# Layers 1 to 3 of a graph network: the adjacency's transpose by block loads and VectorE, the mask and the scaling placed elsewhere in the round

## The chip, the cores and the metric

The kernel runs on one core of a Trainium2 chip. A core has five engines with a queue of instructions each: TensorE (PE, with PEld for its weight loads), VectorE (DVE), ScalarE (ACT), GpSimd (POOL) and SyncE (SP, which here issues nearly all DMAs). They work side by side and wait for each other through semaphores. The metric is the time of one execution on the device in microseconds (us). The kernel before took 3421.11 us, the median of 3 runs (3419.83 to 3423.85).

## The reference

There are 64 graphs of 256 nodes with 256 features in f32, and one adjacency matrix `adj` per graph (256x256, most entries zero, the diagonal kept). Four layers follow each other, and each ends in a residual addition and a layer norm:

```python
# layer 0: a scan over the 256 nodes, a gated recurrence
x = _layernorm(x + _L0_gnn_ref(x, adj, ...), axis=-1)
# layer 1: relu(D^-1/2 adj D^-1/2 (x W^T + b))
degree = jnp.sum(adj_matrix, axis=-1)
norm_adj = adj_matrix * d_inv_sqrt[:, :, None] * d_inv_sqrt[:, None, :]
output = jax.nn.relu(jnp.einsum('bnm,bmo->bno', norm_adj, transformed))
# layer 2: one attention head
att = jax.nn.softmax(scores * mask - NEG * (1.0 - mask), axis=2)
out = jax.nn.relu(jnp.einsum('bnh,ho->bno', jnp.einsum('bnm,bmh->bnh', att, v), Wo) + bo)
# layer 3: eight heads of 32 features, masked where adj is not above 0
scores = jnp.where(adj[:, None, :, :] > 0, scores, jnp.float32(NEG))
attn = jax.nn.softmax(scores, axis=-1)
```

Layer 1's product contracts over the columns of `adj`, and layer 3's scores are kept with keys on the partitions. Both therefore use the transpose of `adj`: layer 1 scaled by `d_inv_sqrt`, layer 3 as a mask.

## The kernel before

Layer 0 is a recurrence over all 64 graphs at once (`_recurrence`). It leaves its states in DRAM as `Hd`, and takes the first 1508 us of the profiled execution. The function `_layers` then does layers 1 to 3 graph by graph. A tile of a graph is 128 partitions by 2 by 256: rows c*128 to c*128+127 are chunk c.

The work is a software pipeline over graphs, written out by hand. A list `ROUND` names steps as `who.step.argument`, and every instruction is issued in that order on its engine; no scheduler changes it (`manual_schedule`). In round `t` the letter tells the graph: L is graph t+1 (degrees, first norm, transpose of `adj`), A is graph t (layer 1), B is t-1 (layer 2), C is t-2 (layer 3 up to the exponentials), E is t-3 (layer 3's output, last norm, store). At the head of round `t` the loads of graph t+2 are issued from SP: `xin` (x), `ad` (adj), `y` (Hd). An engine works through its own queue in order, so an instruction that waits holds all behind it.

Steps that matter here, with lines:

- `residual_0` (L1040): POOL adds `xin` to `y`. `norm_a` (L948 to L952): VectorE's statistics and POOL's power; `norm_b` (L958, L960): VectorE's `shift`, ScalarE's scaling of `y`.
- `degrees_a`, `degrees_b` (L1052 to L1062): row sums of `ad` to the power -1/2, `dis`.
- `adT` (L1064 to L1073), the last but one step of a round: four PE transposes of `ad` into a PSUM bank (`flipped`, L986), two ScalarE activations that scale them into `adT`, and VectorE's mask `neg3`, which reads the same bank.
- `xT` (L1076): PE transposes of `y` and ScalarE's copy. The steps `A.xT.1` and `B.xT.2` open a round and `C.xT.3` stands in its middle.
- `g` (L1085): PE's product with `adT`, ScalarE's relu with `dis`, POOL's addition to `y` (L1092).
- `s2` and `exp2` (L1120, L1130): layer 2's scores, VectorE's `sm` (L1124) and row maximum (L1010), ScalarE's exponentials (L1017).
- `f2` (L1140): a PE product, two VectorE operations from its PSUM bank into the SBUF tile `f` (L1144), a third from `f` and `y` into `y` (L1148).
- `s3` (L1170): for four heads at a time PE's scores, VectorE's addition of the mask (`p`, L1189), ScalarE's exponentials (L1190), and POOL's sum of the two chunks (`p3s`, L1192).
- `o3` (L1196): PE's sums over the keys (L1206, reading `p3s`) and its products with v (L1215), in the order sums of the first four heads, products, sums of the last four. `d3` divides (L1229 to L1231).
- `f3` (L1236): a PE product and VectorE's addition to `y` (L1238). `bias_3` (L1160): SP writes `y` to `Yd`, then POOL adds a bias to `y` (L1162). `store` (L1240) writes the output.

The PSUM banks of `flipped` and `product` are one ring of four (`bank`, L965): a taker waits until the one four before it has been read.

Of the kernel before, what the change touches and what calls it, by code (L numbers as in the profile page):

```python
# [9 lines left out]
F32 = mybir.dt.float32  # L10
BF16 = mybir.dt.bfloat16
AF = mybir.ActivationFunctionType
ALU = mybir.AluOpType
AX = mybir.AxisListType

NEG = 9000000000000000.0
# [3 lines left out]
P = 128  # L20
# [890 lines left out]
def _layers(tc, ident, Hd, Yd, x, adj, weights, out):  # L911
# [8 lines left out]
    nc = tc.nc  # L920
    nat, W2, W3, b1_r, b2_r, b3_r, cols = weights
    B, N, D = x.shape
# [5 lines left out]
    with ExitStack() as ctx:  # L928
# [9 lines left out]
        io = ctx.enter_context(tc.tile_pool(name="l_io", bufs=3))  # L938
# [26 lines left out]
        def bank(name, shape=(P, 2, D)):  # L965
            return ps.tile(list(shape), F32, tag="mm", name=name, bufs=4)

        for c in range(2):
            pt = bank(f"w1_{c}", (P, 2, P))
# [11 lines left out]
        def flipped(src, t):  # L981

            pt = bank(f"tr_{t}")
            for a in range(2):
                for c in range(2):
                    nc.tensor.transpose(  # L986
                        pt[:, a, c * P:(c + 1) * P], src[:, c, a * P:(a + 1) * P], ident
                    )
            return pt

        def product(lhsT, rhs, t):

            pm = bank(f"mm_{t}")
            for c in range(2):
                for k in range(2):
                    nc.tensor.matmul(  # L996
                        pm[:, c, :], lhsT[:, k, c * P:(c + 1) * P], rhs[:, k, :],
                        start=(k == 0), stop=(k == 1),
                    )
            return pm  # L1000

        def new(tag, t, bufs=2, shape=(P, 2, D)):
            return work.tile(list(shape), F32, tag=tag, name=f"{tag}_{t}", bufs=bufs)
# [17 lines left out]
        class Graph:  # L1021
# [7 lines left out]
            def load(self):  # L1029
                b = self.b  # L1030
                self.xin = io.tile([P, 2, D], F32, tag="xin", name=f"xin_{b}")
                nc.sync.dma_start(self.xin, x[b].rearrange("(c p) d -> p c d", p=P))
                self.ad = io.tile([P, 2, N], F32, tag="ad", name=f"ad_{b}", bufs=4)
                nc.sync.dma_start(self.ad, adj[b].rearrange("(c p) m -> p c m", p=P))
                self.y = io.tile([P, 2, D], F32, tag="y", name=f"y_{b}", bufs=7)
                nc.sync.dma_start(self.y, Hd[:, b, :].rearrange("(c p) d -> p c d", p=P))

# [23 lines left out]

                nc.vector.tensor_mul(self.dis, self.dis, self.some)  # L1062

            def adT(self):  # L1064
                pt = flipped(self.ad, f"ad_{self.b}")
                self.adT_sb = new("adT", self.b)
                for c in range(2):
                    nc.scalar.activation(
                        self.adT_sb[:, c, :], pt[:, c, :], AF.Copy, scale=self.dis[:, c:c + 1]
                    )  # L1070

                self.neg3 = new("neg3", self.b, 4)
                nc.vector.tensor_scalar(self.neg3, pt, 0.0, -NEG, ALU.is_le, ALU.mult)  # L1073

            def xT(self, l):
                pt = flipped(self.y, f"x{l}_{self.b}")  # L1076
# [62 lines left out]

            def f2(self):  # L1140
                pm = product(self.pT2_sb, self.w2_sb, f"2f_{self.b}")
                f = new("f2", self.b)
                for c in range(2):
                    nc.vector.scalar_tensor_tensor(  # L1144
                        f[:, c, :], pm[:, c, :], self.sums2[:, c:c + 1], b2_r,
                        ALU.mult, ALU.add,
                    )
                nc.vector.scalar_tensor_tensor(self.y, f, 0.0, self.y, ALU.max, ALU.add)  # L1148


            def qk3(self, s):
# [93 lines left out]
        ROUND = """  # L1245
            A.xT.1 B.xT.2 E.o3 E.d3.0 B.qk2.0 C.norm_b.2 E.d3.1
            A.t B.qk2.1 B.v2 L.residual_0 B.masks L.degrees_a
            E.f3 L.degrees_b C.xT.3 A.g C.bias_3 L.norm_a.0
            C.qk3.0 C.qk3.1 E.norm_a.3 A.norm_a.1 L.norm_b.0 B.s2 B.exp2
            C.s3.0 C.v3 B.w2  # L1250
            B.pT2 E.norm_b.3 E.store A.norm_b.1 C.s3.1 B.f2
            L.adT B.norm_a.2
        """.split()
        graphs = [Graph(b) for b in range(B)]
        graphs[0].load()
        for t in range(-1, B + 3):
            if 0 <= t + 2 < B:
                graphs[t + 2].load()
            for step in ROUND:
                who, name, *args = step.split(".")  # L1260
                b = t - "LABCE".index(who) + 1
# [146 lines left out]
def kernel(ctx: ExitStack, tc: tile.TileContext, ins, out):  # L1408
# [25 lines left out]
    )  # L1434
    Yd = dram.tile([B, P, 2, D], F32, name="Yd")
    found = _layers(tc, ident, Hd, Yd, x, adj, weights, out)
    with tc.If(found > 0):
        _layer_3(tc, ident, Yd, adj, l3, out)
# [36 lines left out]
```

## Time and profile before

| | |
|---|---|
| median of 3 runs | 3421.11 us |
| the profiled execution | 3418.97 us, its span 3417.3 us |
| granted TensorE clock, mean | 0.984 |
| PE busy | 3201.3 us (94%) |
| VectorE busy | 2545.1 us (74%) |
| POOL busy | 1874.6 us (55%) |
| ScalarE busy | 1844.0 us (54%) |
| HBM read, written | 224.01 MB, 99.61 MB |

The profile is of one execution. Its page gives each engine's busy time, the span in 40 equal slices with a digit for the busy tenths, the DMA queues, the chain of work that ended last, and the costliest groups of instructions. The trace behind it can be asked for windows of time, for the chain, and for a timeline, which has a row per run of equal instructions: start in us, length in us, engine, line, operation, output tile, input tiles, shapes and count. A bracket at the end tells how long the engine was idle before and what released it. Consecutive instructions of an engine may overlap by a few hundredths, so a row's length is not exactly the distance to the next one. SPq is SyncE's queue; its rows are the issuing of a DMA, not the transfer.

### The profile page before, as it was taken

The numbers are of one execution on the slowest core, as the hardware profiler recorded it, in microseconds if no ns is written. First come the engines' busy times: TensorE is split into PE (matmuls) and PEld (weight loads), VectorE is DVE, ScalarE is ACT, GpSimd is POOL, SyncE is SP. The second block draws the span as 40 slices with busy tenths as digits, with TensorE's granted clock in tenths as the row PEclk, the third lists the DMA queues.
The fourth block names the chain that finished last, engine by engine and source line by source line (L and its number), as shares of the span: only waits on it lengthen the run. The fifth ranks groups of instructions, "written<-read, shape, count | busy, mean of one in ns | idle before, by whom it ended". The sixth has DMA issues, their size and how long they took to land.

```text
span 3417.3 us, 78895 instructions
## 1 busy us (share of the span) xinstructions
PE 3201.3 (94%) x28840; PEld 2340.6 (68%) x28840; DVE 2545.1 (74%) x7317; ACT 1844.0 (54%) x4754; POOL 1874.6 (55%) x2165
## 2 busy tenths in 40 slices
PE   5799999999889998969999999999999999999997
PEld 4555555555555555547888888888888888888885
DVE  3477777777667777755887888887888878888875
ACT  0255555454444444435666666666666666666664
POOL 2376777776667777743444444444444444444443
PEclk8999999999999999989999999999999999999999
DMA  9756675788876575231111111111111111111100
GB/s 301 228 158 146 162 191 153 171 196 211 205 185 168 152 175 145 57 97 35 46 47 42 44 45 47 47 47 47 47 47 47 47 47 47 47 47 47 47 29 20
DMA packets 389343, 347.82 MB, mean 102 GB/s; under 512 B 107357, under 2 KB 355305, under 8 KB 383721
## 3 DMA queue, kind: packets, MB, share of 16 engines
q1 hardware_dynamic: 371256, 325.82, 35.6%
q10 hardware_dynamic: 17696, 16.91, 1.5%
q8 instruction: 232, 3.80, 0.5%
q14 instruction: 159, 1.29, 0.1%
HBM read 224.01 MB, written 99.61 MB: 95 GB/s over the span
## 4 chain that ended last, share of the span: by engine, by line
PE 75%; DVE 8%; DMA 7%; ACT 3%; SPq 3%; issue 2%; POOL 1%; DVEq 0%; POOLq 0%; ACTq 0%
PE mm L996 13%; PE rc L605 6%; PE rc L597 4%; PE s L1180 4%; PE mm_2f L996 3%; PE mm_t L996 3%; PE mm_3v L996 3%; PE mm_3f L996 3%; PE mm_2v L996 3%; PE mm_g L996 3%; PE mm_2s L996 3%; PE o L1215 3%; DVE ACC L630 3%; PE mm_2w L996 3%; PE late L521 3%; PE o L1206 3%
## 5 line engine op out<-in xcount | busy, mean ns | idle before, releaser
L1192 POOL TENSOR_TENSOR p3s<-p 128x256 f32<-128x256 f32 x512 | 387.4, 788 | 366.6 <-ACT p L1190 366.4
L630 DVE SCALAR_TENSOR_TENSOR ACC<-keep,S,ACC 128x128 f32<-128x128 f32 x1712 | 479.3, 343 | 36.7 <-POOL ACC L875 30.9
L996 PE MATMUL mm<-xT,weights 128*128 128x256 f32 x2048 | 481.8, 383 | 2.9 <-ACT xT L1078 2.9
L996 PEld LDWEIGHTS mm<-xT,weights 128*128 128x128 f32 x2048 | 384.7, 190 | 79.4 <-issue 25.5
L1189 DVE TENSOR_TENSOR p<-s,neg 128x512 f32<-128x512 f32 x512 | 317.7, 683 | 115.3 <-PE s L1180 115.3
L667 POOL TENSOR_TENSOR ACC<-ACC,far 128x384 f32<-128x384 f32 (+1 forms) x313 | 372.3, 1189 | 24.5
L663 POOL TENSOR_TENSOR far<-hs,S 128x384 f32<-128x384 f32 (+1 forms) x313 | 304.9, 974 | 4.7
L960 ACT ACTIVATE y<-y,shift,rstd 128x256 f32<-128x256 f32 x512 | 273.4, 599 | 48.5 <-DVE shift L958 30.7
L1190 ACT ACTIVATE p<-p 128x512 f32<-128x512 f32 x512 | 295.4, 628 | 2.1 <-DVE p L1189 1.6
L805 POOL TENSOR_TENSOR ready<-ACC,dinv 128x128 f32<-128x128 f32 x255 | 102.3, 401 | 310.7 <-DVE ACC L630 310.4
L597 PE MATMUL rc<-WxT,xqT 128*64 128x256 f32 x2048 | 269.3, 384 | 0.0
L1103 ACT ACTIVATE qk<-mm,weights 128x256 f32<-128x256 f32 x256 | 107.5, 471 | 269.1 <-PE mm L996 269.1
L521 PE MATMUL late<-Hw,An 64*32 64x256 f32 x3840 | 215.7, 388 | 30.2 <-ACT lb L256 26.7
L1092 POOL TENSOR_TENSOR y<-y,g 128x512 f32<-128x512 f32 x64 | 81.1, 1267 | 267.6 <-issue 267.6
L1229 DVE RECIPROCAL rT<-o 128x256 f32<-128x256 f32 x128 | 223.8, 1748 | 0.3 <-PE o L1206 0.2
L952 POOL TENSOR_TENSOR rstd<-rstd,mhalf 128x2 f32<-128x2 f32 x256 | 173.8, 697 | 82.3 <-DVE rstd L951 80.6
L948 DVE BATCH_NORM_STATS2 st<-y 128x6 f32<-128x256 f32 x512 | 209.0, 408 | 13.3 <-POOL y L1092 12.5
L605 PE MATMUL rc<-WhT,rT 128*64 128x128 f32 x2048 | 168.9, 286 | 47.9 <-DVE rT L828 47.2
L824 ACT ACTIVATE rs<-rc 128x128 f32<-128x128 f32 x256 | 71.1, 278 | 256.8 <-PE rc L605 256.8
L828 DVE TENSOR_TENSOR rT<-rT_ps,xpT 128x128 f32<-128x128 f32 x256 | 74.3, 290 | 178.8 <-PE rT_ps L826 177.1
L605 PEld LDWEIGHTS rc<-WhT,rT 128*64 128x64 f32 x2048 | 106.8, 136 | 142.3 <-DVE rT L828 126.5
L614 ACT COPY xpT<-xpT_ps 128x128 f32<-128x128 f32 x256 | 68.2, 266 | 245.8 <-PE xpT_ps L612 245.8
(163 smaller groups left out, 7404.8 us busy)
## 6 DMA issues: line engine op xcount, KB each, us to landing
xX<-in_x_dram ACTq DMA_DIRECT2D x16, 1024.0 KB
Us<-xu SPq DMA_DIRECT2D x64, 256.0 KB
xq<-in_x_dram SPq DMA_DIRECT2D x64, 256.0 KB
ACC<-Us SPq DMA_DIRECT2D x32, 512.0 KB
Es<-eu SPq DMA_DIRECT2D x64, 256.0 KB
early_sb<-Es SPq DMA_DIRECT2D x32, 512.0 KB
xin<-in_x_dram SPq DMA_DIRECT2D x64, 256.0 KB
ad<-in_adj_dram SPq DMA_DIRECT2D x64, 256.0 KB
```

What stands on the lines that cost most here:

```text
L521: nc.tensor.matmul(pb[g][q * T:(q + 1) * T, e, :], An[rows, b].rearrange("p u s -> p (u s)"), Hw[rows, b, :], start=True, stop=True,)
L597: nc.tensor.matmul(G[o * B:(o + 1) * B], xqT[a, i // 2][:, i % 2, kc, h * B:(h + 1) * B], WxT[:, kc, o, gates], start=False, stop=False, s ...
L605: nc.tensor.matmul(G[o * B:(o + 1) * B], hT[:, kc * B:(kc + 1) * B], WhT[:, kc, o, g], start=False, stop=(kc == 1), skip_group_check=True,)
L630: nc.vector.scalar_tensor_tensor(acc[:, 0, :], keep[:, j % 2, :], s, acc[:, 0, :], ALU.mult, ALU.add)
L663: nc.gpsimd.tensor_mul(tmp[:, 0:count, :], hs.unsqueeze(1).to_broadcast(shape), s.unsqueeze(2).to_broadcast(shape),)
L667: nc.gpsimd.tensor_add(acc, acc, tmp[:, 0:count, :])
L960: nc.scalar.activation(y[:, c, :], y[:, c, :], AF.Identity, bias=shift[:, c:c + 1], scale=rstd[:, c:c + 1],)
L996: nc.tensor.matmul(pm[:, c, :], lhsT[:, k, c * P:(c + 1) * P], rhs[:, k, :], start=(k == 0), stop=(k == 1),)
L1189: nc.vector.tensor_add(p, s_ps[i], self.neg3)
L1190: nc.scalar.activation(p, p, AF.Exp, scale=ISQ)
L1192: nc.gpsimd.tensor_add(both, p[:, 0, :], p[:, 1, :])
L1229: nc.vector.reciprocal(rT, o_ps[:, 1, :])
```

## The change

`adj` is loaded a second time, as 32x32 blocks set out so that transposing each block in place gives the whole transpose: eight more DMAs per graph, 32 partitions by 8 runs of 128 bytes each, between `ad` and `y`. VectorE transposes the blocks (`adT_v`) and makes the mask from the result in SBUF, in front of `f3`'s addition. ScalarE scales the result into `adT` (`adT_s`) behind `C.xT.3`'s copy. The four PE transposes and their PSUM bank go. The step `adT` leaves the end of the round. In `f2` the two operations write back to the PSUM bank of the product instead of to an SBUF tile, and the third reads that bank.

```diff
                 nc.sync.dma_start(self.ad, adj[b].rearrange("(c p) m -> p c m", p=P))
+                self.az = io.tile([P, 2, 8, 32], F32, tag="az", name=f"az_{b}", bufs=3)
+                for j in range(4):
+                    for a in range(2):
+                        at = a * P + j * 32
+                        nc.sync.dma_start(
+                            self.az[j * 32:(j + 1) * 32, a],
+                            adj[b, :, at:at + 32].rearrange("(i r) c -> r i c", r=32),
+                        )
                 self.y = io.tile([P, 2, D], F32, tag="y", name=f"y_{b}", bufs=7)
...
-            def adT(self):
-                pt = flipped(self.ad, f"ad_{self.b}")
+            def adT_v(self):
+
+                self.turned = new("adTr", self.b)
+                nc.vector.transpose(
+                    self.turned.rearrange("p a m -> p (a m)"),
+                    self.az.rearrange("p a i c -> p (a i c)"),
+                )
+                self.neg3 = new("neg3", self.b, 4)
+                nc.vector.tensor_scalar(self.neg3, self.turned, 0.0, -NEG, ALU.is_le, ALU.mult)
+
+            def adT_s(self):
                 self.adT_sb = new("adT", self.b)
                 for c in range(2):
                     nc.scalar.activation(
-                        self.adT_sb[:, c, :], pt[:, c, :], AF.Copy, scale=self.dis[:, c:c + 1]
-                    )
-
-                self.neg3 = new("neg3", self.b, 4)
-                nc.vector.tensor_scalar(self.neg3, pt, 0.0, -NEG, ALU.is_le, ALU.mult)
+                        self.adT_sb[:, c, :], self.turned[:, c, :], AF.Copy,
+                        scale=self.dis[:, c:c + 1],
+                    )
...
                 pm = product(self.pT2_sb, self.w2_sb, f"2f_{self.b}")
-                f = new("f2", self.b)
                 for c in range(2):
                     nc.vector.scalar_tensor_tensor(
-                        f[:, c, :], pm[:, c, :], self.sums2[:, c:c + 1], b2_r,
+                        pm[:, c, :], pm[:, c, :], self.sums2[:, c:c + 1], b2_r,
                         ALU.mult, ALU.add,
                     )
-                nc.vector.scalar_tensor_tensor(self.y, f, 0.0, self.y, ALU.max, ALU.add)
+                nc.vector.scalar_tensor_tensor(self.y, pm, 0.0, self.y, ALU.max, ALU.add)
...
             A.xT.1 B.xT.2 E.o3 E.d3.0 B.qk2.0 C.norm_b.2 E.d3.1
             A.t B.qk2.1 B.v2 L.residual_0 B.masks L.degrees_a
-            E.f3 L.degrees_b C.xT.3 A.g C.bias_3 L.norm_a.0
+            L.adT_v E.f3 L.degrees_b C.xT.3 L.adT_s A.g C.bias_3 L.norm_a.0
             C.qk3.0 C.qk3.1 E.norm_a.3 A.norm_a.1 L.norm_b.0 B.s2 B.exp2
             C.s3.0 C.v3 B.w2
             B.pT2 E.norm_b.3 E.store A.norm_b.1 C.s3.1 B.f2
-            L.adT B.norm_a.2
+            B.norm_a.2
```

## The prediction

> **What bounds the kernel now.** I read the page first (busy shares, the slices), then the windows of single rounds, then the chain, then the timeline of one round, engine by engine.
>
> ```profile
> span 3417.3 us, 78895 instructions
> ...
> PE   5799999999889998969999999999999999999997
> ...
> PEclk8999999999999999989999999999999999999999
> ```
>
> The recurrence (layer 0) ends near 1508 us; the rest is layers 1 to 3, where PE is full and the granted clock is 1.0. The diff touches that second part alone. One of its rounds, from the windows (columns: PE, PEld, DVE, ACT, POOL busy, clock, DMA share, GB/s):
>
> ```profile
> 2431.00:2459.86 28.86, 28.86 (x197) 23.30 (x198) 23.28 (x57) 18.42 (x40) 13.77 (x17) 1.00 0.14 47
> ```
>
> The L996 row that opens a round stands at 1593.64 and at 3325.76: 1732.1 us, 60 rounds of 28.87. So a round is what counts. In the chain of waits the adjacency's transposes have this place (start, us, what):
>
> ```profile
> 2453.39 1.92 PE mm_2f L996 x8
> 2455.32 0.44 PE tr_ad L986 x4
> 2455.75 0.87 PE tr_x L986 x8
> 2456.62 0.57 PE o L1206 x8
> ```
>
> But "PE busy 28.86" hides a wait. The timeline of a round's end, all engines:
>
> ```profile
> 2455.12 2.19 ACT L1190 ACTIVATE p<-p 128x512 f32<-128x512 f32 x4
> ...
> 2455.89 3.26 POOL L1192 TENSOR_TENSOR p3s<-p 128x256 f32<-128x256 f32 x4 [2.93 <-ACT p L1190]
> ...
> 2456.71 1.15 DVE L1148 SCALAR_TENSOR_TENSOR y<-f,y 128x512 f32<-128x512 f32 x1
> ...
> 2458.52 0.34 PEld L1206 LDWEIGHTS o<-p3s,ones 128*32 128x32 f32 x6
> ...
> 2459.20 0.14 PEld L1206 LDWEIGHTS o<-p3s,ones 128*32 128x32 f32 x2 [0.34 <-POOL p3s L1192]
> ```
>
> PE reaches the last pair of layer 3's row sums at 2458.86 and stands 0.34 us until POOL's fourth `p3s` ends at 2459.15. A round is therefore a loop: PE from there to the end of `mm_2s` (back to back), VectorE's `sm`, ScalarE without a gap from `exp2` to the four `p`, POOL's four `p3s`, PE again. **A shorter PE alone gains nothing; POOL's end must move too.** Cut finer, the third `p3s`:
>
> ```profile
> 2457.27 1.19 POOL L1192 TENSOR_TENSOR p3s<-p 128x256 f32<-128x256 f32 x1
> ```
>
> 1.19 us against a median of 0.73, while L1148 runs on VectorE. L1148 took 0.69 in the first round (1565.19, POOL idle) and 1.15 here. Both read two SBUF tensors; one holds the other up.
>
> **The change, part by part (per round).**
>
> *PE.* The four transposes go: 0.44 us off the stretch in front of the sums.
>
> *f2 in PSUM.* The third operation reads PSUM and one SBUF tensor. Rows of that form (L1189, 128x512) take 0.62 each, four in 2.48, the second four clear of POOL and the first four partly beside POOL's `p3s`, with no difference. So I take 0.69 (uncontended L1148; L1124, PSUM and SBUF, also 0.69) in place of 1.15, and for POOL four `p3s` at the uncontended 2.79 (the round's other four) in place of 3.26: POOL ends 0.48 earlier, at 2458.67. Bounds: 0 (it still collides) and 0.50. The two operations in front now write PSUM: L853 (PSUM out) 359 ns against L866 348, so 0.03 together on VectorE, hidden.
>
> *The loop.* PE would be ready at 2458.86 - 0.44 = 2458.42, POOL is at 2458.67: PE still waits 0.3, and the round shrinks by POOL's 0.48. If POOL came earlier still, PE's own limit would be 0.44 + 0.34 = 0.78; if nothing but PE counted, 0.44.
>
> *adT_v on VectorE.* It gets a 128x512 transpose, of which the trace has no row. Nearest: one-input 128x512 rows (L1052 0.68, L696 0.69); far above, RECIPROCAL, 1748 ns for 256 columns, so 3.5 us. Below nothing is excluded, since it is an added instruction. I take 0.69, the same shape and type with one input. `neg3` from SBUF: 0.69 at most as now (L1073). Together 1.38. The place:
>
> ```profile
> 2438.12 0.17 DVE L1058 TENSOR_SCALAR some<-some 128x2 f32<-128x2 f32 x1
> 2439.84 0.69 DVE L1238 TENSOR_TENSOR y<-y,mm_3f 128x512 f32<-128x512 f32 x1 [1.55 <-PE mm_3f L996]
> ...
> 2447.19 0.69 DVE L1124 TENSOR_TENSOR sm<-mm_2s,ad 128x512 f32<-128x512 f32 x1 [0.86 <-PE mm_2s L996]
> ```
>
> VectorE idles 1.55 just there, and it arrives earlier: `neg3` leaves the round's end (0.69 and a wait of 0.20) and L1148 loses 0.46, 1.35 in all, of which 0.48 is the shorter round. Cover 1.55 + 0.87 = 2.42 against 1.38: cost nothing. Without cover it would hold E's addition, `dis`, ScalarE's `adT_s`, its `g`, POOL's `y`, and at last the `shift` in front of `sm`.
>
> The Trainium skill ("VectorE: DVE Perf Modes", The three transpose paths) gives 311 ns for 128x128 bf16 in 32x32 blocks; four of that, 1.24 us, is an estimate by that page, and its rules for authors send 128x128 transposes to TensorE. By it adT_v is 1.93, still inside 2.42, so the sum stays and only the margin halves.
>
> *adT_s on ScalarE.* 2 x 0.47 in SBUF instead of PSUM, from the round's end (2457.21) to between xT (ends 2440.87) and `g` (2442.01, 1.14 idle before it). `dis` is there at 2440.60. Cost nothing; cover left 0.3, and behind it 0.86 in front of `sm`. What it leaves gives the xT copies 0.8 more room.
>
> *PSUM banks.* One taker less, 16 a round; f2's bank is freed at about 2457.4, its next user four takes on (`t`) starts near 2461. Nothing.
>
> *SP and DMA.* Eight more issues between `ad` and `y`, 256 runs of 128 B each. L269's loads of such runs (`A`) have a median of 0.42 us, so with the gaps 8 x 0.51 = 4.1 us of SP. In a round SP stands idle from 2456.2 to 2463.9, when `Yd` goes out: hidden; behind `Yd` waits POOL's L1162, at 2444.20, 9 us after `Yd`'s 2435.05. The transfer itself, from a stretch of layer 0 of 2 us with almost nothing else:
>
> ```profile
> DMA packets 2505, 0.38 MB, mean 189 GB/s; under 512 B 2493, under 2 KB 2493, under 8 KB 2504
> ```
>
> 2048 runs are so about 1.7 us of a round's 28, beside a DMA share of 0.14.
>
> *The start is where the issues show*, once:
>
> ```profile
> 1509.89 0.46 SPq L1034 DMA_DIRECT2D ad<-in_adj_dram  x1
> 1510.59 0.37 SPq L1036 DMA_DIRECT2D y<-Hd  x1
> ...
> 1515.32 1.26 POOL L1040 TENSOR_TENSOR y<-y,xin 128x512 f32<-128x512 f32 x1 [8.21 <-DMA y<-Hd]
> ```
>
> Graph 0's `y` is issued at about 1514.5 instead of 1510.59. Its data then has no `ad` in front of it, so I take 3.2 of the 3.9 for the landing (bounds 2.5 and 4.1). Against it: `shift` at 1519.53 took 1.21 beside POOL's next L1040, which now comes later (-1.06); `adT` stood in front of xT on ScalarE at 1538.58 (-0.72); at 1564.24 the transposes and `adT` stood in the chain (-0.94). Net +0.5, from -0.2 to +2.5.
>
> **Sum.** 60 rounds x 0.48 = 28.8; the round before them, where PE doesn't wait for POOL, 0.44; the two after the last `ad`, where L1148 still stands beside `p3s`, 0.9; minus 0.5: 29.6 us. The profiled execution took 3418.97 (span 3417.3 and 1.67 around it), so 3389.4. It lay 2.1 under the median of the runs, 3421.11; from the median 3391.5.
>
> **Rivals.**
> 1. *POOL's end does not move* (f2 still collides, or another VectorE instruction takes L1148's place beside `p3s`). PE then waits 0.78 at the sums and rounds stay 28.87: 3421.1 + 0.5 = 3421.6, no change. For it: VectorE's L951, one input, also stretched to 1.28 beside a POOL addition (2442.99). Against: what now follows f2 beside `p3s` is statistics of one input, which keep 0.42 in every row. Chance 0.06.
> 2. *The transpose costs RECIPROCAL's rate*, 3.5 us. adT_v 4.2 against 2.42 makes E's addition 1.8 late; `adT_s` and `g` absorb 0.6, `sm`'s idle time 0.86: 0.35 a round is lost, 21 us: 3412. Chance 0.05.
> 3. *Slower: SP becomes the bound.* If an `az` issue took what `raw`'s took at 141.37, 2.04 us, SP would be at `Yd` at 2472.1, `Yd` would land (2.8 as `xin` did) near 2475.3, and POOL's L1162, due at 2472.6, would be 2.7 late; 0.86 is spare before `sm`: +1.9 a round, 3500. It decides from about 1.86 us an issue on. Against: `A` 0.42, `S` with 328 KB of such runs 0.63; `raw` was issued into full DMA engines, here their share is 0.14. Chance 0.06. The Trainium skill ("DMA: Bandwidth & Descriptors", Specifications) asks for 512 B and more, below which a write becomes read-modify-write; by it this rival would weigh more. The 2493 small packets in 2 us show no such slowness, so I give it no more weight.
>
> **How the numbers follow.** The forecast has 0.81; its own bounds are rounds of 0.44 to 0.50 and a start of +2.5 to -0.2, so 3389 to 3397 from the median, 3387 to 3399 with the spread of the runs (3419.83 to 3423.85). 0.02 remains for what I don't see, on the slow side with rival 3 in part. A measurement tells about 0.2% (7 us) from no change. Faster 0.87 (forecast, rival 2, remainder), same 0.06 (rival 1), slower 0.07. The range reaches a little towards rival 2: 3385 to 3403.
>
> **What would show it.** Right: `tr_ad` gone; rounds of 28.4; L1162 of the new file (f2's third) near 0.69 and four `p3s` near 2.8; PEld still waiting 0.2 to 0.3 on POOL at L1220; transpose and mask done before `mm_3f` ends; ScalarE idle before `g`; SP issues of about 0.45; the first POOL `y` some 3 us later. Wrong: a wait of 0.8 at the sums (rival 1), E's addition waiting for nothing and `sm` late (2), L1176 waiting for `Yd` (3).

## The result and the profile after

The kernel after takes **3390.91 us** (median of 4 runs, 3389.4 to 3393.05), the kernel before, on the same chip, 3422.48 (median of 4, 3419.83 to 3424.96). The ratio is **0.9903, 95% interval 0.989 to 0.9916**: 1% faster. The forecast was 3391.5 in a range of 3385 to 3403.

The profiled execution took 3390.03 (span 3388.2) against 3418.97 before, 28.9 less. By stages, from the rows that bound them in the two traces (the last `hs` of layer 0, and the L996 rows that open rounds):

| stretch | before, us | after, us | difference | forecast |
|---|---|---|---|---|
| to the end of layer 0 | 1507.80 | 1508.87 | +1.1 | 0 |
| start, to the first full round | 85.84 | 86.29 | +0.4 | +0.1 |
| 60 full rounds | 1732.1 | 1700.9 | -31.2 | -28.8 |
| the last three rounds and the end | 91.5 | 92.2 | +0.7 | -0.9 |

So the gain is in the rounds and nowhere else: 28.35 us each instead of 28.87. One round, from the windows of the kernel after (PE, PEld, DVE, ACT, POOL busy with their counts, clock, DMA share, GB/s):

```profile
2417.32:2445.66 28.34, 28.34 (x193) 22.94 (x193) 23.44 (x59) 18.30 (x40) 13.32 (x18) 1.00 0.22 59
```

The DMA share went from 0.14 to 0.22, which is the eight block loads (it is 0.15 in a round of the kernel below that has `f2` in PSUM without them, and 0.22 in the one that has them alone). The end of the same round in the chain of waits, where `tr_ad` is gone:

```profile
2439.74 1.92 PE mm_2f L996 x8
2441.66 0.87 PE tr_x L986 x8
2442.53 0.57 PE o L1220 x8
2443.10 1.73 PE o L1229 x32
2444.83 0.83 PE o L1220 x8
```

And in the timeline, all engines:

```profile
2442.17 2.82 POOL L1206 TENSOR_TENSOR p3s<-p 128x256 f32<-128x256 f32 x4 [2.90 <-ACT p L1204]
...
2443.20 0.69 DVE L1162 SCALAR_TENSOR_TENSOR y<-mm_2f,y 128x512 f32<-128x512 f32 x1
...
2444.43 0.34 PEld L1220 LDWEIGHTS o<-p3s,ones 128*32 128x32 f32 x6
2445.04 0.14 PEld L1220 LDWEIGHTS o<-p3s,ones 128*32 128x32 f32 x2 [0.27 <-POOL p3s L1206]
```

`f2`'s third operation takes 0.69 instead of 1.15 and the four `p3s` 2.82 instead of 3.26; the longest of the 512 `p3s` is now 0.757. The two operations in front of it, which now write PSUM, take 1.01 instead of 0.86, and nothing waits for that. PE still waits for the fourth `p3s`, 0.27 instead of 0.34. VectorE and ScalarE at the place to which the transpose moved:

```profile
2452.62 0.71 DVE L1075 STREAM_TRANSPOSE adTr<-az 128x512 f32<-128x512 f32 x1 [0.20 <-issue]
2453.36 0.43 DVE L1080 TENSOR_SCALAR neg<-adTr 128x512 f32<-128x512 f32 x1
2454.53 0.69 DVE L1252 TENSOR_TENSOR y<-y,mm_3f 128x512 f32<-128x512 f32 x1 [0.74 <-PE mm_3f L996]
```

```profile
2455.45 0.91 ACT L1085 ACTIVATE adT<-adTr,dis 128x256 f32<-128x256 f32 x2
2456.69 0.84 ACT L1104 ACTIVATE g<-mm_g,dis 128x256 f32<-128x256 f32 x2 [0.34 <-PE mm_g L996]
```

The transpose takes 0.71 and the mask 0.43, and VectorE still stands 0.74 us idle in front of E's addition: the work is covered, as is `adT_s`, behind which ScalarE has 0.34 left.

### The profile page after: what moved, and what is told of

Its sections match the earlier page's. It is cut to its first block, busy times and chain, and to the rows that moved or that the text cites. A ratio compares the mean times of both kernels' runs of the same rounds, so it can differ in the third digit from the quotient of the medians.

```text
span 3388.2 us, 78957 instructions
## 1 busy us (share of the span) xinstructions
PE 3173.6 (94%) x28584; PEld 2322.8 (69%) x28584; DVE 2556.4 (75%) x7381; ACT 1837.2 (54%) x4754; POOL 1844.3 (54%) x2165
## 4 chain that ended last, share of the span: by engine, by line
PE 75%; DMA 7%; DVE 7%; ACT 3%; SPq 3%; issue 2%; POOL 1%; DVEq 0%; POOLq 0%; ACTq 0%
PE mm L996 14%; PE rc L605 6%; PE s L1194 4%; PE rc L597 4%; PE mm_2f L996 3%; PE mm_3v L996 3%; PE mm_t L996 3%; PE mm_3f L996 3%; PE mm_2v L996 3%; PE mm_g L996 3%; PE mm_2s L996 3%; PE mm_2w L996 3%; PE late L521 3%; PE o L1229 3%; DVE ACC L630 3%; PE tr_x L986 2%
## 5 line engine op out<-in xcount | busy, mean ns | idle before, releaser
L1206 POOL TENSOR_TENSOR p3s<-p 128x256 f32<-128x256 f32 x512 | 358.3, 731 | 366.0 <-ACT p L1204 365.9
L996 PE MATMUL mm<-xT,weights 128*128 128x256 f32 x2048 | 484.4, 385 | 2.7 <-ACT xT L1093 2.7
L996 PEld LDWEIGHTS mm<-xT,weights 128*128 128x128 f32 x2048 | 387.4, 192 | 79.4 <-issue 25.5
```

Of the source, the lines that this page charges most:

```text
L996: nc.tensor.matmul(pm[:, c, :], lhsT[:, k, c * P:(c + 1) * P], rhs[:, k, :], start=(k == 0), stop=(k == 1),)
L1206: nc.gpsimd.tensor_add(both, p[:, 0, :], p[:, 1, :])
```

## The experiments

"A round" is the mean of 60 from the trace. Layer 0, which no edit touches, ended anywhere between 1505 and 1519 us in the profiled executions, so the rounds tell small differences better than the totals do. In the headings, "after" and "before" are the two kernels. Each ratio is to runs of before on the same chip.

### Which part brought the gain: f2 in PSUM or the transpose?

After, with `f2`'s SBUF tile put back:

```diff
+                f = new("f2", self.b)
...
-                        pm[:, c, :], pm[:, c, :], self.sums2[:, c:c + 1], b2_r,
+                        f[:, c, :], pm[:, c, :], self.sums2[:, c:c + 1], b2_r,
...
-                nc.vector.scalar_tensor_tensor(self.y, pm, 0.0, self.y, ALU.max, ALU.add)
+                nc.vector.scalar_tensor_tensor(self.y, f, 0.0, self.y, ALU.max, ALU.add)
```

> The changed kernel with f2 as it was (third operation from an SBUF tile f); the transposes stay off PE. Theory A (the round is a loop through POOL's p3s, and f2 in PSUM is what moves its end): VectorE's third f2 operation is back at about 1.15 us, four p3s at 3.26, PE waits about 0.8 us at the last row sums instead of 0.27, rounds 28.8 to 28.9 as before the change, total within 5 us of the kernel before. Theory B (PE's transposes were the path, f2 counts for nothing): rounds 28.43, total some 26 us under the kernel before.

Measured: 3417.94 us, ratio to before 0.9985 (0.9976 to 0.9995), a round 28.80. The transposes are off PE, and next to nothing is gained. Timeline of this kernel, end of a round:

```profile
2455.81 3.25 POOL L1207 TENSOR_TENSOR p3s<-p 128x256 f32<-128x256 f32 x4 [2.90 <-ACT p L1205]
...
2456.69 1.09 DVE L1163 SCALAR_TENSOR_TENSOR y<-f,y 128x512 f32<-128x512 f32 x1
...
2459.12 0.14 PEld L1221 LDWEIGHTS o<-p3s,ones 128*32 128x32 f32 x2 [0.55 <-POOL p3s L1207]
```

PE comes 0.44 earlier and stands longer at the last row sums: the bracket has 0.55 instead of 0.34, and the eight matmuls of that group last 1.46 in the timeline instead of 1.08. Those two rows, of this kernel and of before:

```profile
2458.28 1.46 PE L1221 MATMUL o<-p3s,ones 128*32 128x256 f32 x8
```

```profile
2458.74 1.08 PE L1206 MATMUL o<-p3s,ones 128*32 128x256 f32 x8
```

Those 0.38 and the 0.07 that the round did shrink by make up the 0.44. The other half, before with `f2` alone changed:

```diff
                 pm = product(self.pT2_sb, self.w2_sb, f"2f_{self.b}")
-                f = new("f2", self.b)
...
-                        f[:, c, :], pm[:, c, :], self.sums2[:, c:c + 1], b2_r,
+                        pm[:, c, :], pm[:, c, :], self.sums2[:, c:c + 1], b2_r,
...
-                nc.vector.scalar_tensor_tensor(self.y, f, 0.0, self.y, ALU.max, ALU.add)
+                nc.vector.scalar_tensor_tensor(self.y, pm, 0.0, self.y, ALU.max, ALU.add)
```

> The kernel before with only f2 put back to PSUM; adj is still transposed on PE. Theory A: four p3s take 2.8 us, the wait of 0.34 at the last row sums goes, PE then is the limit, rounds 28.53, total some 20 us under the kernel before. Theory B (only PE's own work counts): no change. Theory C (all of POOL's 0.44 counts by itself): rounds 28.43, 26 us.

Measured: 3397.94 us, ratio 0.9926 (0.9909 to 0.9943), a round 28.41. Of the 0.52 that the whole change brings, 0.46 is here. And PE no longer waits; chain of this kernel, then the last row sums in the chain of before:

```profile
2451.98 0.44 PE tr_ad L986 x4
2452.42 0.87 PE tr_x L986 x8
2453.29 0.57 PE o L1205 x8
2453.86 1.73 PE o L1214 x32
2455.59 0.47 PE o L1205 x8
```

```profile
2458.92 0.90 PE o L1206 x8
```

The last row sums take 0.47 here, 0.83 in after and 0.90 in before. That difference is what a late `p3s` costs PE: 0.36 and 0.43, more than the 0.27 and 0.34 that stand in the brackets. Theory A had counted with the bracket's 0.34 and so missed the round by 0.12; the 28.43 of theory C lies nearer, but by it the gain ends with POOL's 0.44 and no other limit, and PE now waits for no `p3s`. The kernel with `norm_b` moved as well, below, tells the two apart.

### If POOL comes still earlier, what are PE's transposes worth?

After, with layer 3's second half of the normalization and its store behind `C.s3.1`, so that ScalarE has two `y` less in front of the second four `p`:

```diff
-            B.pT2 E.norm_b.3 E.store A.norm_b.1 C.s3.1 B.f2
+            B.pT2 A.norm_b.1 C.s3.1 E.norm_b.3 E.store B.f2
```

> The changed kernel with E.norm_b.3 and E.store behind C.s3.1 instead of in front of A.norm_b.1, so ScalarE starts the second four exponentials about 1.0 us earlier. Theory A (POOL's end still holds PE by 0.27): p3s end about 1 us earlier, the wait goes, PE alone is the limit, rounds 28.08, total about 3375. Theory B (PE is the limit already): rounds 28.35, 3391.

Measured: 3368.43 us, ratio to before 0.9846 (0.9829 to 0.9862), a round 27.94. It beats the changed kernel by 0.41 a round, where 0.27 was expected. Timeline and chain of this kernel (POOL waits 2.04 for the second four `p` instead of 2.90, and PE's row sums run through):

```profile
2456.14 2.81 POOL L1206 TENSOR_TENSOR p3s<-p 128x256 f32<-128x256 f32 x4 [2.04 <-ACT p L1204]
...
2459.26 0.35 PEld L1220 LDWEIGHTS o<-p3s,ones 128*32 128x32 f32 x8
```

```profile
2457.36 0.57 PE o L1220 x8
2457.93 1.73 PE o L1229 x32
2459.66 0.43 PE o L1220 x8
```

0.83 less 0.43 is 0.40, the whole gain. The same line was then changed in the kernel with `f2` alone in PSUM, and in before with nothing else.

> The kernel before with f2 in PSUM and, besides, layer 3's norm_b and store behind C.s3.1; PE still transposes the adjacency. Theory A (two limits: POOL's end, and PE's own work): PE is the only limit here, so a round is what f2 in PSUM alone gave, 28.41, PE waits for no p3s, and against the same kernel without PE's transposes (27.94) the transposes are worth 0.47 a round; about 3397. Rival B (norm_b late gains something of its own): a round below 28.3. Rival C (it makes a later wait): above 28.5.

Measured: 3399.31 us, ratio 0.9937 (0.9918 to 0.9955), a round 28.44. Theory A to 0.03: PE is the bound there already, and `norm_b` moved brings nothing more, although POOL's second four `p3s` then begin 0.9 earlier in the round. Against the 27.94 of the kernel that differs only by the adjacency's transpose, that transpose on PE costs 0.50 a round, of which the `tr_ad` rows are 0.44.

> The kernel before with layer 3's norm_b and store behind C.s3.1, and nothing else; f2 stays in SBUF. Theory A: what counts of f2 is only when POOL's p3s end. Layer 3's norm_b in front of f2 is what VectorE and POOL do ahead of it, so POOL's four p3s begin or end earlier by this other means, PE becomes the limit and a round is 28.41, with the third p3s perhaps still 1.19. Rival B (only the collision counts, and it stays): 28.8 to 28.87, 3421.

Measured: 3394.51 us, ratio 0.9926 (0.9904 to 0.9948), a round 28.44. This is one line of the round's order, with `f2` in SBUF, and it brings as much as `f2` in PSUM. Chain, POOL and VectorE of this kernel:

```profile
2469.25 0.44 PE tr_ad L986 x4
2469.68 0.87 PE tr_x L986 x8
2470.55 0.57 PE o L1206 x8
2471.12 1.73 PE o L1215 x32
2472.85 0.43 PE o L1206 x8
```

```profile
2468.90 2.81 POOL L1192 TENSOR_TENSOR p3s<-p 128x256 f32<-128x256 f32 x4 [2.02 <-ACT p L1190]
```

```profile
2471.16 1.09 DVE L1148 SCALAR_TENSOR_TENSOR y<-f,y 128x512 f32<-128x512 f32 x1
```

The collision is still there, but the other way round: the fourth `p3s` was at work when L1148 began, POOL's four keep 2.81, and L1148 is the one that takes 1.09 (6 of the 512 `p3s` of this kernel are still stretched, 63 in before). So it is not the collision as such that made a round 28.87, but POOL's end. Put together, in us a round:

| | POOL late by collision | POOL as after | POOL early (`norm_b` moved) |
|---|---|---|---|
| PE transposes `adj` | 28.87 (before, POOL's end decides) | 28.41 (PE decides) | 28.44 (PE decides) |
| VectorE transposes `adj` | 28.80 (POOL's end) | 28.35 (after, POOL's end) | 27.94 (PE decides) |

### Is the transpose covered, and by what?

The first of three: after, with `adT_v` and `adT_s` put at the end of the round, where `adT` was.

```diff
-            L.adT_v E.f3 L.degrees_b C.xT.3 L.adT_s A.g C.bias_3 L.norm_a.0
+            E.f3 L.degrees_b C.xT.3 A.g C.bias_3 L.norm_a.0
...
-            B.norm_a.2
+            L.adT_v L.adT_s B.norm_a.2
```

> The changed kernel with adT_v and adT_s put where adT stood, at the end of the round in front of B.norm_a.2. Theory A (the place matters): VectorE has the transpose only behind f2, ScalarE's adT waits for it and stands in front of the xT copies, so PE's first product of a round waits about 1.3 us: rounds 29.6, total about 3470. Theory B (the place is free, engines have slack): rounds 28.35, total as the changed kernel, 3391.

Measured: 3446.82 us, ratio 1.0077 (1.006 to 1.0094), a round 29.21. The direction was right, the size was 0.86 a round and not 1.3. Timeline of this kernel:

```profile
2501.99 0.71 DVE L1075 STREAM_TRANSPOSE adTr<-az 128x512 f32<-128x512 f32 x1
...
2502.74 0.91 ACT L1085 ACTIVATE adT<-adTr,dis 128x256 f32<-128x256 f32 x2 [1.09 <-DVE adTr L1075]
...
2503.55 1.05 ACT L1093 COPY xT<-tr_x 128x512 f32<-128x512 f32 x2
...
2504.65 1.99 PE L996 MATMUL mm<-xT,weights 128*128 128x256 f32 x8 [0.93 <-ACT xT L1093]
```

VectorE can start the transpose only behind `f2`, ScalarE waits 1.09 for it with `xT` queued behind, and PE stands 0.93 in front of the next round. The place is therefore worth more than the whole change: 0.86 a round against 0.52. With the operations at the end of the round the kernel is 0.8% slower than before; in the place that the change gave them they cost a round nothing that shows.

The next two do the transpose once or four times more in the same place, into a tile that nobody reads:

```diff
                     self.az.rearrange("p a i c -> p (a i c)"),
                 )
+                for _ in range(1):
+                    spare = new("adTr2", self.b, 1)
+                    nc.vector.transpose(
+                        spare.rearrange("p a m -> p (a m)"),
+                        self.az.rearrange("p a i c -> p (a i c)"),
+                    )
```

> The changed kernel with one more 128x512 transpose on VectorE in adT_v, into a tile that nobody reads (0.71 us). Theory A (cover of 0.74 us idle in front of E's addition): rounds 28.35 to 28.40, total 3391 to 3394. Theory B (VectorE has no cover there): rounds 29.06, total about 3434.

> The changed kernel with four more transposes on VectorE in adT_v, into a tile that nobody reads (2.84 us). Theory A (0.74 of idle time, then 0.34 in front of g and 0.87 in front of sm, all in one line): E's addition 2.1 us late, rounds 29.1, total about 3435. Theory B (nothing behind absorbs it): rounds 30.45, total about 3517. Theory C (VectorE's 4.9 us of idle time in a round absorb it all): rounds 28.35, 3391.

Measured (a single time each): 3386.01 us and a round of 28.35 with one more, 3408.25 and 28.53 with four more (`range(4)`). One more fits into the 0.74. Four more, 2.91 in the row below, are 2.2 too many, and a round lost 0.18 only, where some 0.7 was expected:

```profile
2409.97 2.91 DVE L1081 STREAM_TRANSPOSE adTr<-az 128x512 f32<-128x512 f32 x4
2412.80 0.39 DVE L1086 TENSOR_SCALAR neg<-adTr 128x512 f32<-128x512 f32 x1
2413.11 0.68 DVE L1258 TENSOR_TENSOR y<-y,mm_3f 128x512 f32<-128x512 f32 x1
...
2418.84 0.16 DVE L958 SCALAR_TENSOR_TENSOR shift<-mv,rstd 128x2 f32<-128x2 f32 x1 [0.51 <-POOL rstd L952]
2418.92 0.69 DVE L1145 TENSOR_TENSOR sm<-mm_2s,ad 128x512 f32<-128x512 f32 x1
```

E's addition no longer waits for PE, and `sm` follows the `shift` at once: the idle time in front of both is used up. Against a round of after, E's addition starts 1.8 us later. ScalarE's `g`, with its 0.34 to spare, is 1.25 late; VectorE's L951, which takes 1.27 beside POOL's addition in after (2457.68), takes 0.69 here (2416.25); the `shift` is 1.23 late, and `sm`, with its 0.87 to spare, 0.28 in one round and 0.05 in the next. Only this remainder reaches the round, and rounds of 28.62 and 28.39 alternate. The price that rival 2 had for a slow transpose, 0.35 for an excess of 1.8, was too high for the same reason: 2.2 cost 0.18.

### Is the issuing of the block loads hidden?

After, with the eight block loads once or three times more, into tiles that nobody reads:

```diff
+                for k in range(1):
+                    spare = io.tile([P, 2, 8, 32], F32, tag=f"az{k}", name=f"az{k}_{b}", bufs=1)
+                    for j in range(4):
+                        for a in range(2):
+                            at = a * P + j * 32
+                            nc.sync.dma_start(
+                                spare[j * 32:(j + 1) * 32, a],
+                                adj[b, :, at:at + 32].rearrange("(i r) c -> r i c", r=32),
+                            )
```

> The changed kernel with the eight block loads issued twice, the second time into a tile that nobody reads. Theory A (SP has room in a round): rounds 28.35; the start 2 us longer; total 3393. Theory B (SP or the DMA engines are near their limit): rounds longer by up to 4 us.

> The changed kernel with the eight block loads issued four times, three of them into tiles that nobody reads: 24 more issues of 0.49 us a round. Theory A (SP becomes the bound once Yd is late for POOL's bias addition): Yd goes out some 9 us later, lands 2.2 us after POOL's addition is due, 0.87 of it is spare: rounds 29.7, the start 9 us longer, total about 3485. Theory B (SP never matters in a round): rounds 28.35, total about 3400.

Measured (a single time each): 3394.89 us with 16 loads (a round 28.35, the start 2.3 longer), and 3596.73 with 32 (a round 31.3, from 28.3 to 34.8, and the start 25 longer). With 16 a round feels nothing. With 32 rival 3 of the prediction happens, by number of issues instead of by their length. SyncE's queue of that kernel, and POOL:

```profile
2399.66 0.38 SPq L1264 DMA_DIRECT2D out_dram<-y  x1
2400.10 0.46 SPq L1032 DMA_DIRECT2D xin<-in_x_dram  x1
...
2401.15 4.79 SPq L1039 DMA_DIRECT2D az<-in_adj_dram  x8
2405.99 11.80 SPq L1048 DMA_DIRECT2D az<-in_adj_dram  x24
...
2418.53 0.40 SPq L1184 DMA_DIRECT2D Yd<-y  x1
2430.73 0.38 SPq L1264 DMA_DIRECT2D out_dram<-y  x1
```

```profile
2421.67 1.27 POOL L1185 TENSOR_TENSOR y<-y,weights 128x512 f32<-128x512 f32 x1 [2.42 <-DMA Yd<-y]
```

`Yd` goes out 18.4 us after `xin`, and POOL waits for it. The store `out_dram` of another graph stands behind `Yd` in the same queue and needs ScalarE's last `y`, which runs behind the work that POOL made late; so it goes out only at 2430.73, and the next loads are behind that store. The queue has become a loop of its own, 31.07 from store to store here. The expected 29.7 counted only the lateness of `Yd`, not that SyncE itself then waits for its store. Why the rounds of this kernel are so uneven stays open: single issues of a block load took 1.0 to 1.9 us (65 of 2048), but so did 28 of the 512 in after, whose rounds are even.

### Does the late load of y cost the start?

After, with `y` loaded ahead of the eight:

```diff
                 nc.sync.dma_start(self.ad, adj[b].rearrange("(c p) m -> p c m", p=P))
+                self.y = io.tile([P, 2, D], F32, tag="y", name=f"y_{b}", bufs=7)
+                nc.sync.dma_start(self.y, Hd[:, b, :].rearrange("(c p) d -> p c d", p=P))
                 self.az = io.tile([P, 2, 8, 32], F32, tag="az", name=f"az_{b}", bufs=3)
...
-                self.y = io.tile([P, 2, D], F32, tag="y", name=f"y_{b}", bufs=7)
-                nc.sync.dma_start(self.y, Hd[:, b, :].rearrange("(c p) d -> p c d", p=P))
```

> The changed kernel with y's load issued ahead of the eight az loads. Theory A (the start's delay is SP's issue in front of y): from the recurrence's last hs operation to the first L996 of a full round 86.3 us becomes 84.4, or 85.4 if the shift again stands beside POOL's next addition; rounds 28.35; total 1 to 2 us less. Theory B (the start is bound by something else): 86.3 and no difference.

Measured: 3385.88 us, ratio to before 0.9902 (0.9885 to 0.9918); a round 28.35, the start 82.8 against 86.3, 3.5 shorter and so more than theory A had. The ratio can't be told from that of after; the trace can. POOL's first addition, in after and then here:

```profile
1518.31 1.26 POOL L1048 TENSOR_TENSOR y<-y,xin 128x512 f32<-128x512 f32 x1 [10.13 <-DMA y<-Hd]
```

```profile
1513.32 1.26 POOL L1048 TENSOR_TENSOR y<-y,xin 128x512 f32<-128x512 f32 x1 [7.19 <-DMA y<-Hd]
```

Counted from the end of layer 0 that is 9.4 and 6.5 us. The two edits that helped, together:

```diff
-            B.pT2 E.norm_b.3 E.store A.norm_b.1 C.s3.1 B.f2
+            B.pT2 A.norm_b.1 C.s3.1 E.norm_b.3 E.store B.f2
```

and `y` ahead of the eight as above.

> The changed kernel with both: y's load ahead of the az loads, and E.norm_b.3 and E.store behind C.s3.1. Theory A: rounds 28.08 and a start 1 to 2 us shorter, total about 3373, 1.4% under the kernel before. Theory B (the parts don't add): 3390.

Measured: **3363.15 us, ratio to before 0.984 (0.9827 to 0.9853)**, a round 27.94, the start 84.5. The start gains 1.5 here, against 85.98 with `norm_b` moved alone, and not 3.5. Each start is from one execution, so part of the 3.5 may be no more than the difference between executions. This is the best version of the study: 1.6% under before, where the change itself is 1.0% under it.

## Why the prediction was right, and where its sizes were off

**The bound.** That a round is a loop through PE, VectorE, ScalarE and POOL's `p3s`, and that a shorter PE alone gains next to nothing, held: 28.80 against 28.87 with the transposes gone and `f2` left in SBUF. The 0.07 that did come was put at nothing.

**f2 in PSUM.** "POOL ends 0.48 earlier": 0.44 by the four `p3s` (3.26 to 2.82), with L1162 at 0.69 as taken. That it was the collision with L1148 that stretched the third `p3s` is shown by the pair of kernels that differ in `f2` alone: 3.25 and 2.82, 1.09 and 0.69. The Trainium skill ("SBUF — State Buffer", SBUF: two separate sides) says that a VectorE operation with two SBUF inputs and a GpSimd operation that reads SBUF lock each other out, and that the first to start holds the other up; the trace agrees for both orders, with 1.19 for the `p3s` in before, and 1.09 for L1148 beside an unhindered `p3s` where `norm_b` is moved.

**The round, -0.48.** It was -0.52, by two terms. In the mean of the 60 rounds POOL's second four `p3s` begin 25.00 us after the round's first L996 row and end at 28.27 in before; in after they begin at 24.93 and end at 27.75. So 0.45 is their own length and 0.07 an earlier start, which the prediction did not have. The earlier start goes with the transposes, not with `f2`: 25.00 in before with `f2` alone, 24.94 in after with `f2` in SBUF. It shows on ScalarE, whose first four `p` take 2.43 where PE transposes `adj` and 2.37 where VectorE does. Why they do stays open.

**PE's own limit, 0.44 + 0.34 = 0.78.** This is the term that was mis-sized. With nothing to wait for a round shrinks by 0.93, to 27.94. The 0.34 is the idle time of the weight loads; the row sums' own length, 0.90 in the chain of before, is 0.43 where `norm_b` is moved and nothing waits, and 0.44 + 0.47 = 0.91. The chain of before had the 0.90, and the bracket was read in its stead. It changed nothing in the sum, since POOL stayed the limit, but it made the expectation for the next step 0.14 too small.

**adT_v, 1.38 under 2.42.** Covered, as said; it measured 0.71 + 0.43 = 1.14, since a mask made from SBUF costs 0.43 and not the 0.69 of one read from PSUM. The cover was smaller than said, too: from the end of VectorE's work at 2452.42 to E's addition at 2454.53 there are 2.11 and not 2.42, in part because `f2`'s two operations on PSUM cost 0.15 more and not 0.03. Rival 2 (RECIPROCAL's rate) is out. The 1.24 worked out from the Trainium skill ("VectorE: DVE Perf Modes", The three transpose paths) as an estimate for four 128x128 bf16 blocks lies above the 0.71 of the same area in f32; the measurement decides. The rule of the Trainium skill to do 128x128 transposes on TensorE where PSUM will do ("VectorE: DVE Perf Modes", Rules for kernel authors) would have cost this kernel, whose loads can place the blocks, 0.50 a round once POOL was out of the way (28.44 against 27.94).

**adT_s** free, behind `xT`: 0.91 for both, 0.34 left in front of `g`, against 0.3 said.

**SP, 8 x 0.51 hidden.** They take 3.92 in the round shown (0.49 each; 5.05 in the next one), and a round feels neither 8 nor 16. Rival 3's condition was about 1.86 us an issue, which is some 15 us of SP; the 32 of the round shown took 16.6, and there SP became the bound. The Trainium skill ("DMA: Bandwidth & Descriptors", Specifications) asks for transfers of 512 B and more for the full rate; runs of 128 B cost a round nothing that shows here with 2048 a graph.

**The start, +0.5.** It came out at +0.4, but the first round's 0.44 was to come off too, so it is 0.4 too long. The single terms are less sure than the sum: POOL's first addition came 1.9 later and not 3.2, the `shift` did shrink from 1.21 to 0.16, and the 0.94 of the transposes in front of PE was not to be found as such. Starts of kernels that load alike lie up to 2 us apart (86.29, 86.28, 85.98 and, with one more transpose, 85.62 with the loads as in after; 85.84, 84.27, 86.14 and 86.22 without block loads; 82.79 and 84.46 with `y` first), which is more than the 0.4 in question. That the order of `y` costs some 2 to 3 us, and that about as much is gained elsewhere in the start, agrees with all ten.

**The end, -0.9.** It was +0.7. Of the two rounds that were to get 0.48 shorter each, the first did, 28.33 for 28.85; the second had 27.71 for 27.81. But one group of 16 matmuls took 6.21 where it took 3.72 before, and that is the granted clock, as the last section shows, not the amount of work. Without those 2.5 the end would be at -1.8.

**Rival 1** (POOL's end doesn't move) is excluded by the 512 `p3s` of which none exceeds 0.757.

**The total.** That it came within 0.6 us of the forecast is in part luck. In the two profiled executions the rounds gave 2.4 more than forecast, and the end (1.6), the start (0.4) and layer 0 (1.1) took back that and 0.6 more.

## What to carry to other kernels

When several engines form one loop, list for each what its own limit would be, and treat a change as a pair: here the part in the change's name (transposes off PE) brought 0.07 alone, and 0.50 after another engine had been taken out of the way. Read what a wait costs from the length of the waiting group with and without it, not from the idle time in the bracket alone. And ask of every step that stands in front of a late consumer whether its order can be changed first: moving one normalization behind the scores brought as much alone (0.43) as `f2` in PSUM did (0.46), and with both of the change's parts 0.93 a round.

## What the runs showed of the hardware that was not expected

A transpose in 32x32 blocks of 128x512 f32 took 0.71 us on VectorE, as long as an operation of that size with one input, and a mask read from SBUF 0.43 where the same from PSUM took 0.69.

The granted clock falls near the end of an execution, where PE works in short bursts (in after it stands idle 2.67 and 1.97 us before two rows of `mm_3f` there). The group of 16 L996 matmuls of the last round, in the windows of before (PE, PEld, DVE, ACT, POOL, clock, DMA share, GB/s) and then of after (PE alone, clock, DMA share, GB/s):

```profile
3389.30:3393.10 3.80, 3.72 (x16) 2.96 (x16) 0.78 (x4) 0.86 (x3) 1.45 (x2) 1.00 0.00 0
```

```profile
3359.20:3365.50 6.30, 6.21 (x16) 0.60 0.00 0
```

3.72 / 6.21 is 0.60. The clock fell in before as well, but was back in time: it was granted at 0.50 from 3384.9 to 3388.3, and in after from 3354.1 to 3364.3, through most of the group. All fourteen traces follow this. In eight the fall lasts 10.2 us and covers the start of the group, which takes 5.5 to 6.2 us (after; after with `f2` in SBUF, with one more transpose, with 16 and with 32 loads; the three kernels with `norm_b` moved and `y` not first). In six it lasts 3.4 or 6.8 us and is over when the group begins, which takes 3.7 (before, before with `f2` in PSUM, after with `adT` at the end of the round, with four more transposes, and the two kernels with `y` first). Neither the transpose nor `norm_b` sorts them. What decides how long the fall lasts stays open; it is 2.5 us, more than all that was forecast for the start and the end.
